# Softplus as one activation, and two complex sums formed on TensorE, in the third layer of a four-layer kernel

## The chip, the cores and the metric

The kernel runs on one core of a Trainium2 chip. The metric is the device time of one execution in microseconds; where several runs are given, their median. The engines are called PE (TensorE), DVE (VectorE), ACT (ScalarE), POOL (GpSimd) and SP (SyncE, which here only issues transfers).

## The reference, cut to what matters

The program runs four layers over x of shape (2, 128, 128, 128), each of the form x = x + layer(groupnorm(x)). The change is in the third (layer 2 in the code's numbering). With c = 64, x_r and x_i the two halves of the channels, and two filters A and B given as 7x7 kernels padded and taken to Fourier space:

```python
forget_gate = jax.nn.sigmoid(x_ri @ Wf + bf + 2.0)
input_gate = jax.nn.sigmoid(x_ri @ Wi + bi)
delta = jax.nn.softplus(x_ri @ Wd + bd) * 0.1
...
Bx_r = Br * x_r - Bi_ * x_i
Bx_i = Br * x_i + Bi_ * x_r
inp_r = delta[..., :c] * input_gate[..., :c] * Bx_r
inp_i = delta[..., c:] * input_gate[..., c:] * Bx_i
fg_r, fg_i = (forget_gate[..., :c], forget_gate[..., c:])
def step(h_state, _):
    h_r, h_i = h_state
    Ah_r = Ar * h_r - Ai * h_i
    Ah_i = Ar * h_i + Ai * h_r
    return ((fg_r * Ah_r + inp_r, fg_i * Ah_i + inp_i), None)
(h_r, h_i), _ = jax.lax.scan(step, h0, None, length=T)
```

T is 16. The kernel does not run the 16 steps: the recurrence is linear with constant coefficients for each element, so the sum of the 16 powers of a 2x2 matrix is built by repeated squaring.

## The kernel before, in words

Layer 2 goes through the 16384 positions of both images in 16 steps of 1024 positions. In a step the 128 partitions hold 64 channels of one half (r = 0 real, r = 1 imaginary, as an index in the free dimension) for two runs of 512 positions, and each big tile is 128 x [2 halves r, 2 images, 512], that is 2048 elements per partition; one half of it is 1024, and a tile without r is 1024 as well.

Each step has two parts. `front(i)` makes the gates (`gate`, matmuls into PSUM, then `gated`, an activation with bias per image), the filters (a1 to a11, with `kernels` on PE), the normalised input xn (n1), its product with B (v1 to v4) and with gate and softplus (d7, v5): the input v of the recurrence. `back(i)` forms the power sums on DVE with squares on ACT, and applies them: m1 is v times Ar with the crossed product m2 = v times Ai subtracted (half 0) or added (half 1), then multiplied by f and by b; hv is v times q. `last(r)` adds xh, hv and m1 on PE into PSUM (xs), ACT copies the sum to xh, `measure(r)` takes its statistics on DVE, and for r = 1 the step's result is stored and a later input is loaded by SP. These four end steps of step i run within back(i + 1).

Softplus is built from simple functions: e is |z| (d1), s is relu(z) (d2), e becomes exp(-e) (d3), up is 1 + e (d4), ln is log(up) (d5), c5 corrects e, and d6 adds s + ln - e on PE into the PSUM tile sp, which d7 reads.

The order of the work is written out by hand. `in_order` makes each engine run its instructions in the order in which they are emitted; between engines only data and buffers order them. The loop runs back(i) with front(i + 1) woven between its steps, one for one, and the first steps of front(i + 2) (`lead`) near the end. front returns a list; so does back, in the order of the list.

Buffers count. Pools `one`, `two`, `three` have as many buffers for each tag. PSUM has two buffers for the gates (l2gps), one for the filters aps and bps (l2aps) and one for everything in l2sps: sp0, sp1, xs0 and xs1 before. Among the SBUF tiles of pool `one`, up, xn and m2 share the tag l2up, and ln and hv share l2ln. A new tile of a full tag takes the place of the oldest and waits for that tile's readers.

Lines of the profile that matter: L883 gate, L890 gated, L873 kernels, L898/L901 and L904/L907 square, sum, root and the first use of it, L968 c5, L973 to L975 d6, L978 d7, L984 n1, L991/L994 v1 and v2, L997/L1000/L1003 v3, v4, v5, L1052 and L1061 m1 and m2, L1064 and L1068 the two half sums, L1069 the product with f, L1029 to L1032 last, L1036 measure, L1078 hv, L845/L847 load, L854 load_halves, L864 store.

Of the kernel before, what the change touches and what calls it, by code (L numbers as in the profile page):

```python
# [9 lines left out]
F32 = mybir.dt.float32  # L10
AF = mybir.ActivationFunctionType
ALU = mybir.AluOpType
# [3 lines left out]
P = 128  # L16
NB = 2
# [730 lines left out]
def layer2(tc, cs, ins, x2, x3, stats2, stats3):  # L748
# [7 lines left out]
    nc = tc.nc  # L756
# [3 lines left out]
    with ExitStack() as ctx:  # L760
        pool = lambda name, bufs, **kw: ctx.enter_context(tc.tile_pool(name=name, bufs=bufs, **kw))
        w = pool("l2_w", 1)
# [5 lines left out]
        for j, k in enumerate("fid"):  # L768
            nc.scalar.dma_start(wcat[:, j, :], ins[f"L2_conv_W{k}"])
            h = ins[f"L2_conv_b{k}"]  # L770
            for p0 in (0, HC):
                nc.scalar.dma_start(
                    bcol[p0 : p0 + HC, j, :], bass.AP(h.tensor, h.offset, [[1, HC], [HC, 2]])
                )
        one_col = w.tile([P, 1], F32, name="one_col")
        nc.gpsimd.memset(one_col, 1.0)
        eps_col = w.tile([P, 1], F32, name="eps_col")
        nc.gpsimd.memset(eps_col, 1e-8)
        minus = w.tile([P, P], F32, name="minus")
# [55 lines left out]
        def tile_of(i, name, shape, pl=one, tag=None):  # L835
            held.setdefault(i, {})[name] = t = pl.tile(shape, F32, name=f"{name}_{i}", tag=tag or f"l2{name}")
            return t
# [50 lines left out]
        def gated(i, j, r, out, func):  # L888
            for b in range(NB):
                A.activation(out[:, r, b], held[i][f"g{j}{r}"][:, b], func, bias=bias[:, b, j, r : r + 1])  # L890

        def front(i):

            h = lambda n: held[i][n]

            def a1():
                ps = kernels(i, 0, "aps")
                A.activation(tile_of(i, "sq", [P, 2, N]), ps, AF.Square)  # L898

            def a2():  # L900
                V.tensor_tensor(tile_of(i, "mag", H), h("sq")[:, 0], h("sq")[:, 1], ALU.add)  # L901

            def a3():
                A.activation(h("mag"), h("mag"), AF.Sqrt, bias=eps_col)  # L904

            def a4():
                V.tensor_scalar(tile_of(i, "rec", H), h("mag"), 1e-8, None, ALU.add)  # L907

            def a5():
                V.reciprocal(h("rec"), h("rec"))  # L910

            def a6():
                A.activation(h("mag"), h("mag"), AF.Sigmoid)

            def a7():
                V.scalar_tensor_tensor(h("rec"), h("mag"), 0.95, h("rec"), ALU.mult, ALU.mult)

            def a8():
                V.tensor_tensor(tile_of(i, "ar", [P, 2, N], two), h("aps"), over(h("rec"), 2), ALU.mult)

            def a9():
                A.activation(tile_of(i, "sq", [P, 2, N]), h("ar"), AF.Square)

            def a10():
                V.tensor_tensor(tile_of(i, "al", H, two), h("sq")[:, 0], h("sq")[:, 1], ALU.add)
                kernels(i, 1, "bps")

            def a11():
                A.copy(tile_of(i, "br", [P, 2, N]), h("bps"))

            def f1(r):
                if r == 0:
                    tile_of(i, "f", D, two)
                gated(i, 0, r, h("f"), AF.Sigmoid)

            def i1(r):
                if r == 0:
                    tile_of(i, "ig", D)
                gated(i, 1, r, h("ig"), AF.Sigmoid)

            def d1(r):
                if r == 0:
                    tile_of(i, "e", D)
                gated(i, 2, r, h("e"), AF.Abs)

            def d2(r):
                if r == 0:
                    tile_of(i, "s", D)
                gated(i, 2, r, h("s"), AF.Relu)


            def d3(r):
                if r == 0:
                    nc.scalar.preload_act_table_set("natural_log_exp_and_others")
                A.activation(h("e")[:, r], h("e")[:, r], AF.Exp, scale=-1.0)

            def d4(r):
                if r == 0:
                    tile_of(i, "up", D)
                A.activation(h("up")[:, r], h("e")[:, r], AF.Identity, bias=one_col)  # L960

            def d5(r):
                if r == 0:
                    tile_of(i, "ln", D)
                A.activation(h("ln")[:, r], h("up")[:, r], AF.Ln)

            def c5():
                V.scalar_tensor_tensor(h("e"), h("up"), -1.0, h("e"), ALU.add, ALU.subtract)  # L968

            def d6(r):  # L970
                ps = tile_of(i, f"sp{r}", W, ps_s, "l2sps")
                for b in range(NB):
                    nc.tensor.matmul(ps[:, b], cs.ident, h("s")[:, r, b], start=True, stop=False)  # L973
                    nc.tensor.matmul(ps[:, b], cs.ident, h("ln")[:, r, b], start=False, stop=False)
                    nc.tensor.matmul(ps[:, b], minus, h("e")[:, r, b], start=False, stop=True)  # L975

            def d7(r):
                V.scalar_tensor_tensor(h("ig")[:, r], h(f"sp{r}"), 0.1, h("ig")[:, r], ALU.mult, ALU.mult)  # L978

            def n1(r):  # L980
                if r == 0:
                    tile_of(i, "xn", D, tag="l2up")
                for b in range(NB):
                    A.activation(  # L984
                        h("xn")[:, r, b], h("xh")[:, r, b], AF.Identity,
                        scale=aff[:, r, b, 0:1], bias=aff[:, r, b, 1:2],
                    )


            def v1():  # L990
                V.tensor_tensor(tile_of(i, "v", D, two), h("xn"), both(h("br")[:, 0]), ALU.mult)  # L991

            def v2():
                V.tensor_tensor(h("xn"), h("xn"), both(h("br")[:, 1]), ALU.mult)  # L994

            def v3():
                V.tensor_tensor(h("v")[:, 0], h("v")[:, 0], h("xn")[:, 1], ALU.subtract)  # L997

            def v4():
                V.tensor_tensor(h("v")[:, 1], h("v")[:, 1], h("xn")[:, 0], ALU.add)  # L1000

            def v5():
                V.tensor_tensor(h("v"), h("v"), h("ig"), ALU.mult)  # L1003

            g = lambda j, r: (lambda: gate(i, j, r))
            k = lambda f, r: (lambda: f(r))
            return [
                g(2, 0), k(d1, 0), k(d2, 0), g(2, 1), k(d1, 1), k(d2, 1), k(d3, 0), k(d3, 1),
                k(d4, 0), k(d4, 1), k(d5, 0), k(d5, 1), g(1, 0), a1, c5, a2, k(d6, 0), a3, g(1, 1),
                a4, a6, k(i1, 0), a5, k(d7, 0), k(d6, 1), k(i1, 1), g(0, 0), a7, k(f1, 0), k(d7, 1),  # L1010
                a8, g(0, 1), a9, k(n1, 0), k(f1, 1), a10, a11, k(n1, 1), v1, v2, v3, v4, v5,
            ]

        def back(i):
# [7 lines left out]
            tt, stt = V.tensor_tensor, V.scalar_tensor_tensor  # L1022
            sq = lambda o, a: A.activation(o, a, AF.Square)
            M, AD, SU = ALU.mult, ALU.add, ALU.subtract

            def last(r):
                ps = tile_of(i, f"xs{r}", W, ps_s, "l2sps")
# [6 lines left out]
            def measure(r):  # L1034
# [24 lines left out]
                lambda: (tt(S, p, S, M), sq(q, p)),  # L1059
                lambda: (tt(u, d, u, M), sq(t2, u)),  # L1060
                lambda: tt(tile_of(i, "m2", D, tag="l2up"), x, both(ai), M),  # L1061
                lambda: tt(p, p, u, SU),
                lambda: stt(p, p, 1.0, b, AD, M),
                lambda: tt(v["m1"][:, 0], v["m1"][:, 0], v["m2"][:, 1], SU),  # L1064
                lambda: tt(b, p, q, AD),
                lambda: tt(q, q, d, M),
                lambda: (tt(u, q, t2, SU), sq(q, S), sq(t2, u)),
                lambda: tt(v["m1"][:, 1], v["m1"][:, 1], v["m2"][:, 0], AD),  # L1068
                lambda: tt(v["m1"], v["m1"], f, M),  # L1069
                lambda: tt(S, S, u, SU),  # L1070
                lambda: stt(S, S, 1.0, b, AD, M),
                lambda: tt(b, S, q, AD),
                lambda: tt(q, q, d, M),
                lambda: tt(q, q, t2, SU),
                lambda: tt(t, d, b, M),
# [14 lines left out]
        with in_order(tc):  # L1090
            load(0)
            load_halves(0)
            for i in range(-1, STEPS):
                if i + 2 < STEPS and i >= 0:
                    load(i + 2)
                elif i < 0:
                    load(1)
                    load_halves(1)
                    load_halves(2)

                ahead = [[f] for f in steps_of(i + 1)]
                lead = steps_of(i + 2)
                if i >= 0:
                    ahead[0:10] = [[] for _ in ahead[0:10]]
                if ahead:
                    ahead[-5][:0] = lead[0:6]
                    ahead[-1][:0] = lead[6:10]
                behind = back(i) if i >= 0 else []
                n = max(len(behind), 1)
                for j in range(n):  # L1110
                    if behind:
                        behind[j]()
                    for group in ahead[len(ahead) * j // n : len(ahead) * (j + 1) // n]:
                        for step in group:
                            step()
            for step in held[STEPS - 1]["end"]:
                step()
# [780 lines left out]
```

## Time and profile before

| | |
|---|---|
| Median of 3 runs | 18375.93 us (18361.79 to 18383.79) |
| Span of the profiled execution | 18336.7 us |
| What the median has beyond that span | 39.2 us |
| Layer 2 in the span | 4430 to 5540 us |
| Busy in it, of 1110 us | PE 678.76, DVE 1010.78, ACT 564.71, POOL 1.31 |
| Mean granted TensorE clock in it | 0.81 |

The profile is one execution; its span runs from the first to the last instruction. The page gives no device time of that execution beside the span, so the median of the runs stands for it. Over the whole span DVE is busy for 87%, ACT 81%, PE 78%; most of it is the fourth layer's scan, which the change does not touch. An operation's duration is the mean of its group; two instructions that follow each other on an engine overlap a little, so that start to start is some 0.1 us less than the duration, or just over it when the second needs the first's result.

### The profile page before, as it was taken

The page shows a single profiled execution, that of the slowest core. Times are in us where ns is not written, and L with a number is a line of the kernel's source. Part 1 is how long each engine was busy: PE and PEld are TensorE (multiplying, and loading weights), DVE is VectorE, ACT ScalarE, POOL GpSimd, SP SyncE. Part 2 cuts the span into 40 slices and gives each one's busy share as a digit, 9 for nine tenths or more (in the row PEclk, how much of TensorE's full clock was granted, in tenths as well). Part 3 has the DMA queues.
Part 4 walks back from the last instruction along what each step waited for, and adds up shares of the span by engine and source line. Part 5 has one row for each costly group of instructions (what it writes and reads, how often), then busy time and mean ns, then how long its engine had stood idle before and what let it go on. Part 6 is the DMA issues. An engine that isn't in the chain of part 4 may idle for free. (4 is left out here: it accounts for less than half of the span.)

```text
span 18336.7 us, 277675 instructions
## 1 busy us (share of the span) xinstructions
PE 14346.5 (78%) x97794; PEld 8284.5 (45%) x97794; DVE 15970.0 (87%) x20729; ACT 14905.8 (81%) x30049; POOL 11817.0 (64%) x6490
## 2 busy tenths in 40 slices
PE   7888888887668677777777777777777777777778
PEld 5555555664223344444444444444444444444445
DVE  6776666336999899999999999999999999999996
ACT  4665666334546799999999999999999999999984
POOL 0000000011000599999999999999999999999981
PEclk9999999889889899999999999999999999999989
DMA  2000000121115544444444455544444444445546
GB/s 45 23 24 23 17 18 16 61 65 56 56 51 191 155 116 116 121 127 127 125 116 116 118 127 129 128 121 115 116 125 128 129 125 117 116 119 127 127 131 192
DMA packets 1232638, 1859.32 MB, mean 101 GB/s; under 512 B 124877, under 2 KB 591565, under 8 KB 1228942
## 3 DMA queue, kind: packets, MB, share of 16 engines
q1 hardware_dynamic: 1157374, 1817.40, 37.6%
q10 hardware_dynamic: 73872, 24.16, 0.5%
q8 instruction: 776, 12.71, 0.3%
q14 instruction: 616, 5.05, 0.1%
HBM read 1396.64 MB, written 444.60 MB: 100 GB/s over the span
## 5 line engine op out<-in xcount | busy, mean ns | idle before, releaser
L1625 DVE TENSOR_TENSOR_SCAN hs<-da,states,ups 128x512 f32<-128x512 f32 x8192 | 9931.7, 1265 | 255.4 <-PE ups L1617 238.7
L1643 POOL TENSOR_TENSOR hs<-hs,cb 128x2048 f32<-128x2048 f32 x2048 | 9399.9, 4590 | 318.0 <-POOL but L1580 198.6
L1617 PE MATMUL ups<-ident,but 128*128 128x128 f32 x32768 | 5560.5, 301 | 2617.4 <-DVE hs L1625 1715.1
L1617 PEld LDWEIGHTS ups<-ident,but 128*128 128x128 f32 x32768 | 3859.2, 150 | 6207.6 <-DVE hs L1625 3515.8
L1585 ACT ACTIVATE but<-du,bt 128x256 f32<-128x256 f32 x12800 | 5350.7, 500 | 4.5 <-DVE du L1466 4.2
L1561 ACT ACTIVATE da<-db,na 128x512 f32<-128x512 f32 x8192 | 5238.6, 713 | 18.6 <-DMA db<-dd 15.8
L1599 PE MATMUL yps<-hs,sel 128*32 128x512 f32 x16384 | 2482.5, 682 | 50.4 <-POOL hs L1643 44.3
L1580 POOL TENSOR_TENSOR but<-du,bt 128x256 f32<-128x256 f32 x3584 | 2148.5, 619 | 17.0 <-DVE du L1466 17.0
L306 POOL TENSOR_TENSOR xres<-xres,rowb 128x256 f32<-128x256 f32 x128 | 94.3, 737 | 2440.3 <-DMA xres<-in_x 1744.7
L391 ACT COPY pT<-tps 128x512 f32<-128x512 f32 x1280 | 723.6, 585 | 1104.3 <-PE tps L386 1104.1
L386 PE MATMUL tps<-ident,s 128*128 128x128 f32 x8192 | 1223.7, 286 | 437.4 <-DVE pT L389 271.0
L358 DVE CUSTOM_DVE_ANT_1 s<-sps,relbias 128x512 f32<-128x512 f32 x2048 | 1321.7, 683 | 133.2 <-PE sps L341 127.9
L386 PEld LDWEIGHTS tps<-ident,s 128*128 128x128 f32 x8192 | 896.4, 143 | 1029.4 <-issue 498.5
L371 ACT ACTIVATE s<-s,nm 128x1024 f32<-128x1024 f32 x1024 | 1166.2, 1141 | 126.8 <-DVE nm L369 124.1
L1156 POOL MEMSET xpad<- 128x34 f32 x8 | 1.3, 162 | 1170.1 <-PE xs L1030 1105.8
L341 PE MATMUL sps<-kc,qT 32*128 32x512 f32 x4096 | 614.7, 668 | 1.9 <-DVE qT L326 1.2
L1637 ACT COPY states<-hs 128x4 f32<-128x4 f32 x2048 | 384.4, 188 | 247.5 <-DVE hs L1625 247.5
L389 DVE COPY pT<-tps 128x512 f32<-128x512 f32 x768 | 528.1, 688 | 55.9 <-PE tps L386 53.2
L1599 PEld LDWEIGHTS yps<-hs,sel 128*32 128x32 f32 x16384 | 339.4, 114 | 476.1 <-issue 301.9
L1349 PE MATMUL xdps<-xc,xpw 128*40 128x512 f32 x1024 | 540.8, 610 | 12.4 <-POOL xd L1286 12.4
L734 POOL TENSOR_TENSOR xr<-xr,row_ln_b 128x512 f32<-128x512 f32 x64 | 81.2, 1271 | 708.2 <-DMA xr<-x 474.7
L1381 PE MATMUL dtps<-xd,dtw 65*128 65x512 f32 x1024 | 534.0, 603 | 0.0
(287 smaller groups left out, 16171.3 us busy)
## 6 DMA issues: line engine op xcount, KB each, us to landing
db<-dd SPq DMA_DIRECT2D x1024, 512.0 KB
cb<-cd SPq DMA_DIRECT2D x1024, 256.0 KB
xc<-xs SPq DMA_DIRECT2D x256, 512.0 KB
dd<-dl SPq DMA_DIRECT2D x256, 512.0 KB
ut<-xst SPq DMA_DIRECT2D x128, 512.0 KB
yc<-ysb SPq DMA_DIRECT2D x128, 512.0 KB
yf<-yc SPq DMA_DIRECT2D x128, 512.0 KB
ys<-yt SPq DMA_DIRECT2D x128, 512.0 KB
```

Of the source, the lines that this page charges most:

```text
L341: nc.tensor.matmul(sps, v["qT"][hp, qt * P : (qt + 1) * P], kc[b, wh + g][hp, ww : ww + 2].rearrange("p a r c -> p (a r c)"), start=True, ...
L358: nc.vector.tensor_tensor_reduce(blocks(v["s", qt][:, h, 512 * g : 512 * g + 512]), blocks(v["sps", qt, g][h]), bias[:, h, :, r0 : r0 + WS ...
L371: nc.scalar.activation(s[:, h, :], s[:, h, :], AF.Exp, bias=nm[:, 2, h : h + 1], scale=-1.0, accum_out=v["sums"][:, qt, h : h + 1],)
L386: nc.tensor.transpose(tps[:, j, :], v["s", qt][:, h, k0 : k0 + P], cs.ident)
L391: nc.scalar.copy(dst, tps)
L1561: nc.scalar.activation(da[:, j, :], held[i]["db"][:, 4 * e + j, :], AF.Exp, scale=na[:, k, c : c + 1])
L1580: nc.gpsimd.tensor_tensor(but[:, j, :, n, :], du[:, tb], bt[:, tb, c : c + 1].unsqueeze(2).to_broadcast([P, 8, 32]), ALU.mult,)
L1585: nc.scalar.activation(but[:, j, :, n, :], du[:, tb], AF.Copy, scale=bt[:, tb, c : c + 1])
L1599: nc.tensor.matmul(v["yps"][e][32 * j : 32 * j + 32, :], sel, hs[:, j, :], start=(q == 0), stop=(q == 3),)
L1617: nc.tensor.transpose(ups[:, tb * P : (tb + 1) * P], v[("but", q, tb // 2)][:, tb % 2, 4 * e + j].rearrange("p n c -> p (n c)"), cs.ident,)
L1625: nc.vector.tensor_tensor_scan(o, a, u, state[:, c0 + j : c0 + j + 1], ALU.mult, ALU.add)
L1643: nc.gpsimd.tensor_tensor(hs, hs, v["cb"][:, s // 2, :].unsqueeze(1).to_broadcast([P, 4, T]), ALU.mult)
```

## The change

Softplus becomes one activation, AF.Softplus, written to e; d2 to d6, c5 and their tiles go, and d7 reads e from SBUF. A new helper `cross` forms a[r] -/+ b[1 - r] on PE: the identity times one half, and the identity or its negative times the other half of the crossed product, added in PSUM. v3 and v4 become vs(0), vs(1) with it, and the subtraction and addition on m1 become ms(0), ms(1). v5 and the product with f are done by halves, reading these PSUM tiles. kernels(i, 1) becomes a step of its own, kb, and both lists are put in a new order; the lead is now four steps, all at the end of the step.

```diff
-        one_col = w.tile([P, 1], F32, name="one_col")
-        nc.gpsimd.memset(one_col, 1.0)
...
+        def cross(i, name, a, b, r):
+            ps = tile_of(i, name, W, ps_s, "l2sps")
+            for n in range(NB):
+                nc.tensor.matmul(ps[:, n], cs.ident, a[:, r, n], start=True, stop=False)
+                nc.tensor.matmul(
+                    ps[:, n], cs.ident if r else minus, b[:, 1 - r, n], start=False, stop=True
+                )
...
             def a10():
                 V.tensor_tensor(tile_of(i, "al", H, two), h("sq")[:, 0], h("sq")[:, 1], ALU.add)
+
+            def kb():
                 kernels(i, 1, "bps")
...
             def d1(r):
                 if r == 0:
                     tile_of(i, "e", D)
-                gated(i, 2, r, h("e"), AF.Abs)
...
+                gated(i, 2, r, h("e"), AF.Softplus)
 
             def d7(r):
-                V.scalar_tensor_tensor(h("ig")[:, r], h(f"sp{r}"), 0.1, h("ig")[:, r], ALU.mult, ALU.mult)
+                V.scalar_tensor_tensor(h("ig")[:, r], h("e")[:, r], 0.1, h("ig")[:, r], ALU.mult, ALU.mult)
...
-            def v3():
-                V.tensor_tensor(h("v")[:, 0], h("v")[:, 0], h("xn")[:, 1], ALU.subtract)
-
-            def v4():
-                V.tensor_tensor(h("v")[:, 1], h("v")[:, 1], h("xn")[:, 0], ALU.add)
-
-            def v5():
-                V.tensor_tensor(h("v"), h("v"), h("ig"), ALU.mult)
+            def vs(r):
+                cross(i, f"vs{r}", h("v"), h("xn"), r)
+
+            def v5(r):
+                V.tensor_tensor(h("v")[:, r], h(f"vs{r}"), h("ig")[:, r], ALU.mult)
...
             return [
-                g(2, 0), k(d1, 0), k(d2, 0), g(2, 1), k(d1, 1), k(d2, 1), k(d3, 0), k(d3, 1),
-                k(d4, 0), k(d4, 1), k(d5, 0), k(d5, 1), g(1, 0), a1, c5, a2, k(d6, 0), a3, g(1, 1),
-                a4, a6, k(i1, 0), a5, k(d7, 0), k(d6, 1), k(i1, 1), g(0, 0), a7, k(f1, 0), k(d7, 1),
-                a8, g(0, 1), a9, k(n1, 0), k(f1, 1), a10, a11, k(n1, 1), v1, v2, v3, v4, v5,
+                g(2, 0), k(d1, 0), g(2, 1), k(d1, 1), g(1, 0), a1, a2, a3, g(1, 1),
+                a4, a6, k(i1, 0), a5, k(d7, 0), k(i1, 1), g(0, 0), a7, k(f1, 0), k(d7, 1),
+                a8, kb, k(n1, 0), a11, k(n1, 1), v1, v2, k(vs, 0), g(0, 1), a9, k(f1, 1),
+                k(v5, 0), k(vs, 1), a10, k(v5, 1),
             ]
...
+            def ms(r):
+                cross(i, f"ms{r}", v["m1"], v["m2"], r)
+
+            def mf(r):
+                tt(v["m1"][:, r], v[f"ms{r}"], f[:, r], M)
...
                 lambda: tt(tile_of(i, "m2", D, tag="l2up"), x, both(ai), M),
-                lambda: tt(p, p, u, SU),
+                lambda: (ms(0), tt(p, p, u, SU)),
                 lambda: stt(p, p, 1.0, b, AD, M),
-                lambda: tt(v["m1"][:, 0], v["m1"][:, 0], v["m2"][:, 1], SU),
                 lambda: tt(b, p, q, AD),
                 lambda: tt(q, q, d, M),
                 lambda: (tt(u, q, t2, SU), sq(q, S), sq(t2, u)),
-                lambda: tt(v["m1"][:, 1], v["m1"][:, 1], v["m2"][:, 0], AD),
-                lambda: tt(v["m1"], v["m1"], f, M),
+                lambda: (mf(0), ms(1)),
                 lambda: tt(S, S, u, SU),
                 lambda: stt(S, S, 1.0, b, AD, M),
                 lambda: tt(b, S, q, AD),
+                lambda: mf(1),
...
                 if i >= 0:
-                    ahead[0:10] = [[] for _ in ahead[0:10]]
+                    ahead[0:4] = [[] for _ in ahead[0:4]]
                 if ahead:
-                    ahead[-5][:0] = lead[0:6]
-                    ahead[-1][:0] = lead[6:10]
+                    ahead[-1][:0] = lead[0:4]
```

More of the change, by code (lines that the diff above doesn't have):

```diff
@@ L943, in d1 @@
                     tile_of(i, "e", D)
-                gated(i, 2, r, h("e"), AF.Abs)
[L946 to L975, printed above, removed]
+                gated(i, 2, r, h("e"), AF.Softplus)
             def d7(r):
-                V.scalar_tensor_tensor(h("ig")[:, r], h(f"sp{r}"), 0.1, h("ig")[:, r], ALU.mult, ALU.mult)
+                V.scalar_tensor_tensor(h("ig")[:, r], h("e")[:, r], 0.1, h("ig")[:, r], ALU.mult, ALU.mult)
             def n1(r):
```

## The prediction

> **What bounds the kernel now.** I read the windows view first, because the change lies in the third layer alone: its instructions run from 4430 to 5540 us of the span.
>
> ```profile
> core 0: us, PE busy (x) PEld busy (x) DVE busy (x) ACT busy (x) POOL busy (x), PEclk, DMA share, GB/s
> 4430.00:5540.00 1110.00, 678.76 (x1824) 242.68 (x1824) 1010.78 (x784) 564.71 (x688) 1.31 (x7) 0.81 0.18 51
> ```
>
> This stage is 1110 us, 6% of the span, and DVE is busy for 1011 of them; PE and ACT have room. What counts is therefore DVE's queue: the instructions on it and the times it waits. The waits of the same window say who makes DVE wait (waited for, by whom: total, times, longest), and what PE waits for:
>
> ```profile
> PE xs L1030 <- DVE hv L1078: 215.2, 16, 28.3
> ...
> DVE ig L978 <- PE sp L975: 28.1, 16, 5.0
> ...
> DVE rec L907 <- ACT mag L904: 13.5, 16, 1.3
> DVE mag L901 <- ACT sq L898: 12.1, 8, 1.7
> ```
>
> Leaving out the first step's shares (4.98, 1.34 and 0.51 us), a steady step has 23.1/15 + 12.2/15 + 11.6/15 = 3.1 us of DVE waits. Steps begin 65.4 and 67.7 us apart in turn (hv L1078 starts at 4606.76, 4672.19, 4739.88), 66.6 on average. PE spends 12 us a step waiting for DVE. The groups of the window give the prices (form, count, busy, mean ns):
>
> ```profile
> L968 DVE SCALAR_TENSOR_TENSOR e<-up,e 128x2048 f32<-128x2048 f32 x16 | 36.6, 2285 | 13.9 <-ACT up L960 13.9
> ...
> L997 DVE TENSOR_TENSOR v<-v,xn 128x1024 f32<-128x1024 f32 x16 | 19.5, 1220 | 0.0
> L919 DVE TENSOR_TENSOR ar<-aps,rec 128x1024 f32<-128x1024 f32 x16 | 19.5, 1218 | 0.0
> ...
> L954 ACT ACT_TABLE_LOAD x16 | 20.5, 1283 | 0.3
> ```
>
> Last, the timeline of PE around one restart, and the waits of the DMA queue:
>
> ```profile
> 4742.22 2.07 PE L1030 MATMUL xs<-hv,ident 128*128 128x512 f32 x2 [12.21 <-DVE hv L1078]
> 4744.09 1.91 PE L1031 MATMUL xs<-m,ident 128*128 128x512 f32 x2
> 4745.80 1.51 PE L1029 MATMUL xs<-xh,ident 128*128 128x512 f32 x2
> 4747.14 1.02 PE L1030 MATMUL xs<-hv,ident 128*128 128x512 f32 x2
> ```
>
> ```profile
> SPq L847 <- PE bps L873: 816.9, 15, 64.0
> ```
>
> A pair of 128x512 records costs 0.86 us from start to start at full clock (4747.14 to 4748.00) and 1.7 to 1.9 when the granted clock is 0.50, as after this 12 us gap. The queue line shows a rule of this program: a tile whose tag has one buffer (tab) is not written until the last reader of the tile it replaces is done, even where that reader (bps) is emitted later than the request.
>
> **What leaves DVE.** Per step c5 (L968) and the four half sums v3, v4, L1064, L1068 go: start to start 2.20 + 1.14 + 1.26 + 1.13 + 1.22 = 6.9 us. v5 and the multiplication by f become two halves each, about 0.1 us more per pair. That a sum is read from PSUM costs nothing: L919 reads PSUM at 1218 ns, L997 reads SBUF at 1220. d7 now reads SBUF: 1.19 to 1.22. Net -6.8. The old 3.1 us of waits go too: sp exists no longer, and mag and rec get new places.
>
> **What leaves ACT and PE.** ACT loses Relu, Exp, Identity and Ln, 9.4 us a step by the means of their groups (716 ns x4, 1050 x2, 1143 x2, 1055 x2), but is busy only half the time: nothing by itself. Softplus takes the place of Abs (701 ns), same form, PSUM source and bias. Table loads stay three a step, each 1.283 us: softplus, square root, sigmoid, where it was log/exp, square root, sigmoid. If softplus could not share its table with Copy and Square it would be one more; on the path that matters only between the copy of xs1 and the root, 1.3 us a step, 14 x 1.3 = 18 us. PE loses 24 records of sp and gains 32 of the four cross products, with 12 us of slack a step. The memset and kernels(1) as its own step kb cost nothing: kb still runs between a8 and a11 with 4 us to spare, and SP's tab load, which waits for it, comes no later.
>
> **Where DVE waits after the change.** All six uses of the one l2sps buffer (xs0, xs1, ms0, ms1, vs0, vs1) now follow each other: each waits until the one before is read. I wrote out the order in which each engine gets its instructions and followed it with the row durations. Four places wait.
>
> W1, square root's input. PE's queue from the end of v5(0) is vs1, the next step's g20 and g21, xs0 of the step just ended, g10, aps. At full clock: 4 pairs 3.44 + two gates 3.5 (8 records took 1.77) + 6 pairs 5.15 + 1.75 + 1.75 + 0.2, then ACT's square 1.01 + 0.1: 16.9 us. DVE has beside it qq, hv, a10, v5(1), t, two products and d, two stats: 11.1 us, and then stands at mag (a2). Wait 5.8. Before, hv alone released xs0, and the gates stood ahead of it.
>
> W2, rec (a4). From a2's start, DVE has 0.6 + 2.20 + 1.25 + 1.25 = 5.3. ACT's queue: the copy of xs1 stands ahead of the root. xs1 ends 4.1 us after a2 starts (5.15 + 0.2 from the end of aps, 1.2 of which lie before a2); copy 1.01, table load 1.28, root 0.72: 7.2. Wait 1.9.
>
> W3, v1. m2 and xn share one buffer (tag l2up). In the old order m2's last reader was L1068, a DVE instruction placed ahead of n1. Now it is ms1 on PE, which waits for mf(0) to read ms0, and n1(0) stands before ms1 in the text but, by the tab line, must wait for it. Behind n1(0) on ACT stand a11 and n1(1), and v1 needs all three. From the end of mf(0): ms1 3.44 + 0.2, n1 1.43, br 0.92, n1 1.51, 0.2: 7.6; DVE has only two 1.2 us instructions. Wait 5.2.
>
> W4, v5(0). vs0 starts after mf(1), when PE has idled some 11 us, so at half clock: two to four of its pairs at 1.7, 5.2 to 6.9 with latency, against 5.7 us of DVE work. 0 to 1.2; I take 0.5, since the quoted restart had three slow pairs.
>
> [...]
>
> [...]
>
> **Sum.** Waits 5.8 + 1.9 + 5.2 + 0.5 = 13.4; less 3.1 of old waits and 6.8 of work: +3.5 us a step. 14 full steps give +49. The first front has no cover: its c5, v3, v4 and the 4.98 us wait for sp go (9.7), two crosses on the chain come (at most 5): -5. The last step has no next front: two half sums go, -2. Total +42, rounded to +40: the same walk of the old order gives steps of 65.3 and 67.9 us where the trace has 65.4 and 67.7, so a tenth or two a step stays open. The profiled span is 18336.7; the median is 18375.9, so 39.2 us lie around it, unchanged. 18376.7 of span, 18416 us in all, +0.22%.
>
> **Rivals.** A, about no change: W3 is not paid in full, for instance if n1 finds its buffer free. Without W3 a step is 3.5 - 5.2 = -1.7, at most 14 x -1.7 - 7 = -31; part comes back, because vs0 then starts earlier after less cover: about 18360. For it: the walk has slack that I cannot see. Against: the tab line.
>
> B, faster: DVE stays the only bound and every wait is hidden, since PE has 12 us of idle a step. The 6.8 us of DVE work go 16 times: 18376 - 109 = 18267. It decides if PE's queue runs ahead of DVE by over 6 us at v5(1), that is if the gates did not stand between vs1 and xs0. Against: one buffer forbids running ahead.
>
> [...]
>
> **How the numbers follow.** About 0.2% (37 us) is what a measurement of this kernel tells from no change, so the forecast, at +40, lies just over the line. Forecast 0.60 (0.48 above the line, 0.12 below), A 0.21, B 0.12, C 0.07. Slower 0.48 + 0.07 = 0.55, same 0.12 + 0.21 = 0.33, faster 0.12. The forecast's own range, W1 and W3 each off by one microsecond, W4 between its bounds, is 18385 to 18445. With most of A the range is 18360 to 18448, leaving out B and C, 0.19.
>
> **What would show it.** DVE waits at mag behind the square of aps (about 4 us after a stats wait of 2), at rec behind the root (1.9), at v1 behind xn (5.2), a little at v5(0). hv's starts 70 us apart. ACT waits for PE's ms1 at n1. Softplus at 0.7 us, three loads a step. If v1 does not wait and hv stands 66 us apart, A is right; at 60, B.

## The result, and the profile after

The changed kernel takes 18467.18 us (median of 4 runs, 18447.94 to 18475.81) against 18379.86 us for the kernel before beside it (4 runs, 18361.79 to 18410.53): a ratio of 1.0049, 95% interval 1.0034 to 1.0063. It is slower by 87 us. The forecast was slower by 40 us with a range up to 18448: the sign was right, the size was short by half.

Where the time lies can be read from two marks that both kernels have: the bias of the second image, with which the third layer's steps can begin, and the last statistics. "The layer" is the time between them in what follows. It is 1105.4 us before and 1168.1 us after; in a second profile of each, 1104.2 and 1169.1. So the layer is 63 to 65 us longer. The other 22 to 24 us lie outside it. In the profiles what is longer behind the layer is the fourth layer's scan, which the change does not touch (by 42 us in the first pair of profiles, by 25 in the second); the last experiments return to it.

The windows view of the changed kernel over exactly its layer (time, then busy us of PE, PEld, DVE, ACT and POOL with counts, granted clock, DMA share, GB/s):

```profile
4455.70:5623.80 1168.10, 776.06 (x1920) 266.40 (x1920) 902.96 (x731) 436.28 (x528) 0.50 (x5) 0.81 0.17 48
```

DVE's busy time falls as forecast: by the same view over the layer of the kernel before it is 1009.22 us, now 902.96, 6.6 us less a step. But DVE's idle time in the layer rises from 96 to 265 us. Who makes it wait stands in the waits view (waited for, by whom: total, times, longest):

```profile
PE vs L893 <- DVE m L1004: 162.2, 15, 10.8
...
DVE v L968 <- ACT xn L961: 85.2, 16, 6.2
...
DVE stats L1016 <- ACT xh L1012: 71.3, 17, 8.4
...
DVE mag L907 <- ACT sq L904: 44.5, 16, 9.2
ACT xn L961 <- PE ms L894: 44.5, 15, 3.0
...
DVE rec L913 <- ACT mag L910: 29.5, 15, 2.0
...
DVE v L977 <- PE vs L894: 27.3, 32, 4.6
```

The four DVE instructions that the prediction named are all there: v1 (L968), mag (L907), rec (L913) and v5 (L977). The line with stats is a part of W1's wait, as the timeline of one steady step shows (start, duration, instruction, and in brackets the idle time ahead and who ended it):

```profile
4838.28 1.22 DVE L977 TENSOR_TENSOR v<-vs,ig 128x1024 f32<-128x1024 f32 x1 [1.15 <-PE vs L894]
...
4840.67 2.29 DVE L1057 TENSOR_TENSOR hv<-v,q 128x2048 f32<-128x2048 f32 x1
...
4843.78 1.23 DVE L977 TENSOR_TENSOR v<-vs,ig 128x1024 f32<-128x1024 f32 x1 [0.22 <-PE vs L894]
...
4853.75 1.30 DVE L1016 BATCH_NORM_STATS2 stats<-xs 128x6 f32<-128x512 f32 x2 [3.97 <-ACT xh L1012]
4857.42 0.69 DVE L907 TENSOR_TENSOR mag<-sq 128x512 f32<-128x512 f32 x1 [2.37 <-ACT sq L904]
...
4864.72 0.43 DVE L913 TENSOR_SCALAR rec<-mag 128x512 f32<-128x512 f32 x1 [2.01 <-ACT mag L910]
...
4896.30 2.29 DVE L968 TENSOR_TENSOR v<-xn,br 128x2048 f32<-128x2048 f32 x1 [5.29 <-ACT xn L961]
...
4912.34 2.29 DVE L1057 TENSOR_TENSOR hv<-v,q 128x2048 f32<-128x2048 f32 x1
```

From hv to hv (L1057) the step takes 71.67 us. Its waits are 5.29 at v1, 1.15 + 0.22 at the halves of v5, 3.97 + 2.37 at stats and mag, and 2.01 at rec: 15.0 us, where the prediction had 13.4. With 66.6 - 3.1 - 6.8 + 15.0 = 71.7 the step adds up; no other term is needed.

The timeline of PE shows the restart that was costed from the old trace:

```profile
4831.55 2.04 PE L893 MATMUL vs<-v,ident 128*128 128x512 f32 x2 [10.81 <-DVE m L1004]
4833.39 1.91 PE L894 MATMUL vs<-xn,minus 128*128 128x512 f32 x2
4835.09 1.92 PE L893 MATMUL vs<-v,ident 128*128 128x512 f32 x2
4836.80 1.44 PE L894 MATMUL vs<-xn,minus 128*128 128x512 f32 x2
4838.17 1.94 PE L881 MATMUL g<-xT,wg 128*64 128x512 f32 x8
4840.04 1.12 PE L893 MATMUL vs<-v,ident 128*128 128x512 f32 x2
```

After 10.81 us without work not only three but all four pairs of vs0 run slowly. The fourth takes 1.37 us to the next start, between a slow pair's 1.71 and a fast one's 0.86, so that full clock came back within it. The granted clock (the number behind POOL's count) in the windows view puts that at 4837.64, 6.1 us after the restart:

```profile
4831.55:4837.64 6.09, 6.09 (x7) 2.49 (x8) 5.55 (x4) 0.00 (x0) 0.00 (x0) 0.50 0.01 3
4837.64:4868.30 30.66, 25.83 (x82) 8.92 (x80) 21.32 (x20) 15.62 (x19) 0.00 (x0) 1.00 0.11 34
```

From the groups (form, count, busy us and mean ns, idle time ahead):

```profile
L888 ACT ACTIVATE e<-g,bias 128x512 f32<-128x512 f32 x64 | 40.5, 684 | 53.3 <-PE g L881 53.3
```

Softplus is a single activation of 684 ns; the same view has three groups of 16 table loads, three a step as before, at 1283 ns each. A half of v5, which reads PSUM, takes 1224 ns (L977).

### The profile page after: what moved, and what is told of

Read it like the earlier page. It is cut to its first block, busy times and chain, and to the rows that moved or that the text cites. A ratio compares the mean times of both kernels' runs of the same rounds, so it can differ in the third digit from the quotient of the medians.

```text
span 18461.4 us, 277738 instructions
## 1 busy us (share of the span) xinstructions
PE 14513.0 (79%) x97922; PEld 8345.4 (45%) x97922; DVE 15880.8 (86%) x20681; ACT 14741.1 (80%) x29889; POOL 11821.4 (64%) x6489
```

## The experiments

Five kernels undo one thing each or do one part alone, one joins three of these, and three move the scan that follows. Layer and steps are from the profile of each; the times are medians with the number of runs, against the kernel before on the same chip in the same hour. The kernels before and after were also profiled once more.

> The kernel before once more, for its profile. The two profiles at hand differ by 125 us of span, but only 63 us of it lie between the first gate matmul and the last statistics of the third layer; 22 lie in the two layers before it and 40 in the fourth, which the change does not touch. Theory S (scatter): these 62 us are how executions differ, and a second profile of the kernel before shows its third layer within 2 us of the first one's 1105 us, with steps of 65.4 and 67.7 us, while the other layers move by tens of us. Rival F (far effect): the change slows the other layers, and this profile agrees with the first one in every layer within 5 us.

> The changed kernel once more. Theory S: third layer 1168 us again, steps of 71.68 us; the other layers within the scatter of the kernel before; time 65 to 90 us above the kernel before. Rival F: the fourth layer again 40 us longer than in every profile of the kernel before.

| kernel | median us (runs) | before | ratio, 95% interval | layer us | steady step us |
|---|---|---|---|---|---|
| before, again | 18363.81 (1) | 18355.92 | | 1104.2 | 65.42 and 67.69 in turn |
| after, again | 18447.94 (4) | 18355.92 | 1.0050 (1.0035 to 1.0065) | 1169.1 | 71.68 |
| own_buffer | 18348.49 (10) | 18355.92 | 0.9997 (0.9988 to 1.0007) | 1116.6 | 68.27 |
| softplus_only | 18385.83 (10) | 18355.92 | 1.0014 (1.0005 to 1.0023) | 1109.8 | 68.27 |
| gates_early | 18326.99 (10) | 18375.44 | 0.9976 (0.9967 to 0.9985) | 1068.4 | 64.85 |
| root_first | 18388.12 (10) | 18375.44 | 1.0008 (0.9999 to 1.0017) | 1096.7 | 66.03 and 67.10 in turn |
| keep_warm | 18439.09 (4) | 18375.44 | 1.0039 (1.0025 to 1.0053) | 1144.0 | 69.85, at times 70.2 |
| all_three | 18249.69 (5) | 18375.44 | 0.9932 (0.9919 to 0.9946) | 981.9 | 58.4 to 60.5 |

Two profiles of one kernel agree in the layer to 1.2 us, so the layer column separates the kernels far better than the medians do. Outside the layer they agree less: in the second profile of the kernel before the third layer begins 26 us later than in the first, and in that of the changed kernel the scan is 16 us shorter than in the first. So theory S holds for the layer, and rival F, 40 us more in the fourth layer each time, does not: it is 42 and then 25. The time, 92 us above the kernel before, is just over the 65 to 90 of theory S.

**A buffer of its own for xn** (W3). Only the tag of xn is changed, so that n1 need not wait for ms1, the last reader of m2:

```diff
-                    tile_of(i, "xn", D, tag="l2up")
+                    tile_of(i, "xn", D)
```

> The changed kernel with xn in a buffer of its own, so that n1 need not wait for ms(1). Theory W (waits along the one order): the 5.3 us wait of v1 behind xn goes and the others stay, at most 1 or 2 us of it come back at v5(0), because the cover before it is shorter; steps of 66.5 to 68.5 us, 45 to 70 us faster than the changed kernel, that is 15 us on either side of the kernel before. Rival R (the clock's raster): the step sits at 71.68 us, 21 times 3.413 us, because the granted clock changes only at such marks; it goes to a whole number of marks, 68.27 us if one is gained, else it stays. Rival P (PE is full): taking the wait away gives nothing, as PE's queue is the bound.

The layer falls from 1169 to 1117 us, still 11 us above the kernel before, and the time is level with it. The step of 68.27 us lies in theory W's range and is also rival R's mark, so this run does not decide between the two. DVE's waits, in the waits view from 4600 to 5400 us (12 steps):

```profile
DVE v L968 <- ACT xn L961: 26.3, 12, 2.2
...
DVE v L977 <- PE vs L894: 11.8, 24, 0.8
```

v1's wait falls from 5.29 to 2.19 a step, by 3.1 and not by 5.2. The rest has another cause, which the timeline of ACT shows:

```profile
4804.53 1.06 ACT L997 ACTIVATE q<-S 128x1024 f32<-128x1024 f32 x1 [8.79 <-DVE u L1046]
...
4806.44 1.51 ACT L961 ACTIVATE xn<-xh,aff 128x512 f32<-128x512 f32 x2
```

n1 (L961) no longer waits for PE, but starts directly behind two squares of back(i), and these stand in ACT's queue behind DVE's u (8.79 us of idle). The buffer was the wait that came last; the place in ACT's queue is the next one. The shared tag costs 3.4 us a step (71.68 to 68.27) and 52 us of the layer. Of the 3.4 us, 3.1 come at v1 and 0.3 at v5 (1.38 to 1.06), because vs0's slow stretch is 5.6 us here instead of 6.1 by the granted clock.

**The gate and the lead earlier** (the part of W1 that the gates add, and W4). The gate g01 with its two users is issued before v1 instead of behind vs0, and the lead (the first four steps of the front after next) six groups of steps earlier:

```diff
-                a8, kb, k(n1, 0), a11, k(n1, 1), v1, v2, k(vs, 0), g(0, 1), a9, k(f1, 1),
-                k(v5, 0), k(vs, 1), a10, k(v5, 1),
+                a8, kb, k(n1, 0), a11, k(n1, 1), g(0, 1), a9, k(f1, 1), v1, v2, k(vs, 0),
+                k(v5, 0), k(vs, 1), a10, k(v5, 1),
...
-                    ahead[-1][:0] = lead[0:4]
+                    ahead[-7][:0] = lead[0:4]
```

> The changed kernel with its last gate (g01, with its sigmoid f1) and the four lead steps (both softplus gates of the next step) moved from around vs(1) into PE's 10.8 us pause before vs(0). Theory W: the two gates (3.5 us) leave the chain from v5(0) to mag, and vs(0) no longer starts cold, which takes the 1.2 + 0.2 us at v5: 71.68 - 4.9 = 66.8 us a step, 70 us faster than the changed kernel; the wait of v1 (5.3) stays. With the raster the step settles on the mark below, 64.85, or on 68.27. Rival P (what counts is the number of matmuls, or the one buffer): no change, since not one matmul or buffer is taken away.

The layer is 1068.4 us, 101 less than after the change, and the kernel is faster than before by 0.24% (0.15 to 0.33). The waits in the same view:

```profile
DVE mag L907 <- ACT sq L904: 28.4, 12, 2.4
...
DVE stats L1016 <- ACT xh L1012: 23.0, 13, 1.8
DVE v L968 <- ACT xn L961: 18.1, 12, 1.5
```

Stats waits 1.8 us a step instead of 4.0, v1 1.5 instead of 5.3, v5 0.4 instead of 1.4; mag and rec are as they were. Since an issue order was moved, several things move at once: the gates no longer stand between vs1 and xs0, g01 fills a part of PE's pause, and v1 comes later against the rest of back(i). This run shows what the order is worth in all, not how it divides among the three. The expectation had v1 keep its wait; it lost 3.8 us of it, so the step reached 64.85, the mark named, by another sum than the one expected. This is the largest gain of the five.

**The root ahead of xs1's copy** (W2). end[2], which issues xs1 and its copy, moves two places down:

```diff
                 end[1],
-                end[2],
                 lambda: tt(tile_of(i, "m1", D, two), x, both(ar), M),
                 lambda: tt(u, u, d, SU),
+                end[2],
```

> The changed kernel with the copy of xs1 placed behind the square root on ACT (end step 2 two places later in the list; PE's order stays). Theory W: only W2 goes, the 2.0 us of rec behind mag: 69.7 us a step, 28 us faster in all; on the raster either 71.68 (nothing) or 68.27 (48 us). The waits at mag (2.4), v1 (5.3) and the stats (4.0) stay. Rival P: nothing.

The wait at rec is gone from the view, and with it nearly all of mag's, which was not meant:

```profile
DVE v L968 <- ACT xn L961: 64.6, 12, 7.3
...
DVE mag L907 <- ACT sq L904: 2.1, 12, 0.2
```

mag waits 0.18 us a step instead of 2.37. In DVE's timeline m1's product (L1031, 2.27 us) now stands between the stats and mag, where it covers the rest of the chain through xs0, g10, aps and the square; in ACT's, the root comes before the copy of xs1. Two terms of the prediction, W2 and the end of W1, thus hang on one position in the list. v1 keeps its wait (5.2 in the steady steps). The steps, 66.03 and 67.10 in turn, are below all that was expected, since mag's wait went as well. The layer is 1096.7 us, below that of the kernel before, yet the median is 13 us above it (0.9999 to 1.0017, no verdict): in the profile the scan is 11707 us here, against 11675 and 11676 in the kernel before.

**PE kept busy in its pause** (W4). The gate g01 is computed five more times into its own PSUM tile before vs0, work without use, there to keep the clock up:

```diff
-                a8, kb, k(n1, 0), a11, k(n1, 1), v1, v2, k(vs, 0), g(0, 1), a9, k(f1, 1),
+                a8, kb, k(n1, 0), lambda: (a11(), again(i, 0, 1, 5)), k(n1, 1), v1, v2, k(vs, 0),
+                lambda: again(i, 0, 1, 1), a9, k(f1, 1),
```

(again issues the eight matmuls of the gate so many times.)

> The changed kernel with nothing moved; g01 is computed five more times into its own PSUM tile in PE's 10.8 us pause before vs(0) (the last time where it stood), work for nothing, so that PE does not stand still there. Theory C (clock): vs(0) then runs at full clock, 3.6 instead of 6.7 us; the waits at v5 (1.2 and 0.2) go and the step falls by 1.4 us or to the next mark: 70.3 or 68.27 us, 20 to 48 us faster with 40 more matmul records a step. Rival P: PE's queue is the bound, and 8.7 us of matmuls more make the step longer by as much. Rival N: the clock plays no part, nothing changes.

PE's timeline in this kernel:

```profile
4814.49 8.80 PE L893 MATMUL g<-xT,wg 128*64 128x512 f32 x40
4825.37 2.04 PE L905 MATMUL vs<-v,ident 128*128 128x512 f32 x2 [2.08 <-DVE m L1017]
4827.21 1.79 PE L906 MATMUL vs<-xn,minus 128*128 128x512 f32 x2
4828.84 1.02 PE L905 MATMUL vs<-v,ident 128*128 128x512 f32 x2
```

The pause ahead of vs0 is 2.08 us instead of 10.81, two pairs are slow instead of four, and DVE has no wait left at v5. In this step vs0 takes 5.3 us up to g01's start, which DVE's own work covers. By the windows view from 4600 to 5500 us the mean granted clock is 0.90, against 0.81 in the changed kernel. Steps take 69.96 us on average (979.45/14) instead of 71.6; the waits at v1, stats, mag and rec hardly change (5.19, 3.97 or 3.79, 2.37, 2.01). So the slow stretch of vs0 costs 1.65 us a step, 24 us of the layer, which is then 39 us longer than before.

**Softplus alone.** The single activation stays; v3, v4, v5 and the two half sums return to DVE as before:

```diff
-            def vs(r):
-                cross(i, f"vs{r}", h("v"), h("xn"), r)
+            def v3():
+                V.tensor_tensor(h("v")[:, 0], h("v")[:, 0], h("xn")[:, 1], ALU.subtract)
...
-                lambda: (mf(0), ms(1)),
+                lambda: tt(v["m1"][:, 1], v["m1"][:, 1], v["m2"][:, 0], AD),
+                lambda: tt(v["m1"], v["m1"], f, M),
```

> The kernel before with softplus as one activation and nothing on PE for the sums (v3, v4, v5 and the two half sums on DVE as before; kernels(1) stands behind a10 as before; the first four steps of the next front where the first six stood). By DVE's queue alone each step loses c5 (2.2 us) and the waits for sp (1.5): 62.9 us a step, 55 us faster than before. Theory R (raster): PE now has long pauses, restarts at half clock, and the step settles on a multiple of 3.413 us: 68.27 us, slower than before by about 10 us in all, although work left every engine. If so, half of the loss of the change is not in the crosses. Rival Q: softplus as an activation is slower than 0.7 us or needs a fourth table load.

Taking c5 and the wait for sp from DVE does not make the layer shorter (1109.8 against 1104 to 1105 us), for a new wait takes their place:

```profile
DVE mag L907 <- ACT sq L904: 76.3, 12, 6.6
```

mag waits 6.4 us a step. Its input comes through aps, and in this shorter list aps stands behind xs1's six pairs in PE's queue, where after the whole change it stands ahead of them. The step was expected at 68.27 and is 68.27, though the expectation did not rest on this wait. A restart at half clock, which it did name, stands in the same chain, at the head of xs0:

```profile
4817.61 2.07 PE L1012 MATMUL xs<-hv,ident 128*128 128x512 f32 x2 [14.92 <-DVE hv L1060]
```

Its first three pairs take 5.2 us to the next start (4822.78) instead of three times 0.86, so the restart can account for up to 2.6 us of the 6.4, an estimate; no run took the two apart. What follows is bounded: softplus in this place in the order brings nothing. That it would bring nothing in any order was not tried.

**The three repairs together:** own buffer, gates early and root first.

> Own buffer for xn, gates early and root first together. Theory W: of the waits 5.3 (v1), 2.0 (rec), 1.4 (v5) and 3.5 of the 6.4 (stats and mag) go: 71.68 - 12.2 = 59.5 us a step, or 61.44 us (18 marks) on the raster; 140 to 170 us faster than the changed kernel, 18280 to 18310 us, so about 60 us below the kernel before. DVE would then be busy nearly throughout. Rival P: not below the kernel before, since the crosses on PE cost what they save on DVE.

This kernel is faster than either theory had it: 18249.69 us, 0.68% faster than before (0.54 to 0.81). Its steps, 59.2 us on average, are near the 59.5 of theory W's sum and do not settle on the 61.44 of the raster. The windows view over its layer, and DVE's waits from 4600 to 5400 us:

```profile
4467.10:5449.00 981.90, 736.64 (x1920) 249.79 (x1920) 898.83 (x730) 433.34 (x528) 0.50 (x5) 0.89 0.20 57
```

```profile
DVE stats L1016 <- ACT xh L1012: 24.8, 14, 1.8
DVE m L1004 <- PE ms L894: 8.9, 8, 2.1
DVE mag L907 <- ACT sq L904: 2.3, 13, 0.2
DVE v L977 <- PE vs L894: 2.0, 1, 2.0
```

DVE's busy time is that of the changed kernel (898.83 against 902.96 us), and the layer is 186 us shorter. Of 15.0 us of waits a step some 2.8 are left (38.0 us in the 13.5 steps of the view). So the edits to the arithmetic do pay, once little waits for them. A better order alone could not have done it: the kernel before has 63 us of DVE work in a step (1009.22/16), more than the 59.2 us that a step takes here.

**Does the scan's time hang on its start?** The scan of the fourth layer takes 11674.7 and 11676.0 us in the two profiles of the kernel before, 11716.2 and 11700.5 in those after. All other stages behind the layer agree within 3 us. Three kernels add 14 or 28 additions on DVE behind the third layer:

```diff
             for step in held[STEPS - 1]["end"]:
                 step()
+            for _ in range(14):
+                V.tensor_tensor(held[STEPS - 1]["hv"], held[STEPS - 1]["hv"], held[STEPS - 1]["m1"], ALU.add)
```

> The kernel before with 14 additions of 128x2048 on VectorE after the last step of the third layer (on tiles that nobody reads again), about 14 x 2.2 = 31 us that only delay what follows. Question: why the fourth layer's scan, which no kernel here touches, takes 11674.7 and 11676.0 us in the two profiles of the kernel before, 11716.2 and 11700.5 in those of the changed one, and 11661.8 to 11708.2 in the others. Theory P (the scan's length hangs on the moment at which it starts): the scan leaves 11674 to 11677 by 8 us or more. Theory Q (it hangs on what the third layer leaves behind, its program or its tiles): the scan stays within 11674 to 11677, and the whole is 18376 + 31 = about 18407 us.

> As the kernel with 14 additions, with 28 of them: about 62 us of delay, which brings the scan's start to about where it is in the changed kernel. Theory P: the scan differs from 11675 by 8 us or more, and from that of the kernel with 14 additions. Theory Q: it stays within 11674 to 11677, the whole about 18438 us.

> The changed kernel with the same 14 additions (31 us) after its third layer. Theory P: the scan leaves 11700 to 11716. Theory Q: it stays within 11700 to 11716, the whole about 18464 + 31 = 18495 us.

| kernel | median us (runs) | before | delay us | scan us |
|---|---|---|---|---|
| before + 14 | 18392.13 (10) | 18366.23 | 32 | 11672.3 |
| before + 28 | 18428.01 (6) | 18366.23 | 65 | 11646.1 |
| after + 14 | 18470.45 (4) | 18366.23 | 31 | 11694.0 |

Neither theory holds as it was put. A start 32 us later leaves the scan of the kernel before alone (11672.3), one 65 us later gives a scan 29 us shorter in the profiled execution, and the changed kernel's, 31 us later, is 6 us below the lower of its two others. But the execution with the scan 29 us shorter, at 18391.9 us, is the shortest of six; the other five lie between 18419.78 and 18438.67, which fits a scan of the usual length. So executions of this one program differ by 28 to 47 us, and in the profiled one it is the scan that is short, while its third layer is as long as ever (1105.7 us). The two layers ahead scatter as well: the third begins between 4433.9 and 4467.1 us over all the profiles, with no relation to the kernel. By medians the changed kernel has 22 to 27 us outside the layer in two comparisons and 8 in the third (18470.45 - 18366.23 - 65 - 31). Over the variants of the changed kernel the scan runs from 11661.8 (own_buffer) to 11708.2 us (keep_warm). What makes it longer, and whether it always is, stays open; the profiles do not show that the change does it.

## Why the prediction was right or wrong, point by point

Measured in the steady step of the changed kernel, in us:

| step of the prediction | forecast | measured |
|---|---|---|
| work off DVE | -6.8 | -6.6 by busy time of the layer, -6.8 by step and waits |
| W1, stats and mag | 5.8 | 6.3 |
| W2, rec | 1.9 | 2.0 |
| W3, v1 | 5.2 | 5.3 |
| W4, v5 | 0.5 (0 to 1.2) | 1.4 |
| all waits | 13.4 | 15.0 |
| step against before | +3.5 | +5.1 |
| first front | -5 | -6 |
| last step | -2 | -2 and 0 in the two pairs of profiles |
| layer | +42, rounded to +40 | +63 to +65 |
| outside the layer | 0 | +22 to +24 |

**Right:** the mechanism, and all four places. W3 rested on one line of the DMA queue's waits (816.9 us in 15 waits), which showed that in this program a tile of a full tag waits for a reader that is issued later. It is the longest wait at one instruction; own_buffer shows that the tag is 3.1 us of it, and that the rest has another wait right behind it. W2 and W3 came out to 0.1 us from row durations and a written order (W3's terms add up to 7.7 and not 7.6, which makes it the 5.3 measured). Softplus at 0.7 us (684 ns), three loads of 1283 ns and the cost of reading PSUM (1224 ns for a half of v5) were as costed. ACT hardly stands idle ahead of a load: at the root and the sigmoid there are 16 loads each with 0.3 us of idle time ahead in total.

**Wrong, the term of the sum that was mis-sized: W4.** It was bounded at 0 to 1.2, for two to four slow pairs, and set to 0.5, for the three of the one restart quoted, where full clock came back after 4.55 us. In the steady step v5(0) waits 1.15, the upper bound, and v5(1) another 0.22: vs0 is four pairs long and lies wholly inside a slow stretch of 6.1 us. The length of this stretch is not fixed. Over the runs it goes from 3.4 (keep_warm) to 6.2 us (root_first), and the wait at v5 goes with it (the stretch is counted from vs0's start until the granted clock is full again; the first step is that between the first two hv):

| run, step | vs0 at half clock, us | wait at both halves of v5, us |
|---|---|---|
| root_first, every other steady step | 3.54 | 0.22 |
| own_buffer, first step | 4.67 | 0.57 |
| changed kernel, first step | 5.24 | 0.94 |
| own_buffer, steady step | 5.62 | 1.06 |
| root_first, the steps between | 5.80 | 1.19 |
| changed kernel, steady step | 6.11 | 1.38 |

For a stretch of 4.55 us the 0.5 was thus about right; what failed was to take the length from one restart. In the trace of the kernel before, others lasted 4.0 and 5.7 us. W4 is 0.9 of the 1.6 us that the waits of a step are over the forecast, 12 us of the layer.

Half a microsecond more, 7 us of the layer, is **W1**. Its chain was let start at the end of v5(0), but g01 stands between vs0 and vs1 in PE's queue: v5(0) ends at 4839.50, vs1 starts at 4840.04. This is not an effect of the clock, for in keep_warm stats and mag wait 3.97 and 2.37 us as well. That run takes the waits at v5 away, and the step falls to 69.96 us, where the forecast with W4 at nothing would be 69.6. The 24 us of the layer that it saves are what vs0's slow stretch costs in all, of which the forecast had 7.

**Wrong in a detail that cost nothing:** W1's split. The forecast had 2 us at stats and 4 at mag; it is 3.97 and 2.37. The statistics of xs start only when ACT's copy of the same PSUM tile has ended (copy at 4852.71 for 1.01 us, stats at 4853.75), which the walk let run side by side. mag waits for PE's chain anyway, so the sum of both is what the chain gives.

**Wrong, without effect on the difference:** the 39.2 us put "around the span". The profiled execution of the changed kernel took 18463.18 us with a span of 18461.4: 1.8 us lie around a span. The rest was the difference between two executions.

**Wrong, a term put at nothing without a reason:** the time outside the layer. The sum adds the layer's 40 us to the span and leaves the rest as it was. There lie 22 to 24 of the 47 us that the forecast falls short by, as much as the layer's terms together, and with the layer's 63 to 65 us alone the time would have been inside the range. No run shows what causes it. The range allowed for none of it, since it was made of the layer's terms alone, although the three times before already spread over 22 us. It was also added up too narrow: W1 and W3 off by 1 us each and W4 at its bounds, all at once, make 18381 to 18454, not 18385 to 18445.

**The rivals.** A (W3 not paid in full) fell: n1 waits 3.0 us on ACT for ms1, and v1 5.3. own_buffer is what A supposed, and it lands near A's no change (18348, ratio 0.9997), but not by A's sum: that had a step 1.7 us shorter than before, and it is 1.7 longer, the layer 11 us longer. B (all waits hidden) was to be decided by whether PE runs ahead of DVE at v5(1); the change does not let it. all_three, with three things changed, comes to 18250, near B's 18267. C (a cold restart in W1's chain) fell: PE does not idle before vs1, and the one restart that DVE waits for is vs0's, which the forecast had itself as W4.

## What to carry to other kernels

When sums move from VectorE to TensorE, write down every engine's queue in the new order, and cost each tile's wait for the last reader of the tile whose buffer it takes, even where that reader is issued later: here 6.6 us of VectorE work saved a step became 5 us lost, and one tag alone cost 3.4 of them. Before such a change is given up, move the waiting work in the queues; the same arithmetic with one buffer more and three places in the order changed is 0.7% faster than the kernel before. A short TensorE job behind a long pause is costed by the longest slow stretch that the traces show (6.2 us here), not by one example, and together with what stands between it and the next job that counts. And terms "outside the change" get a width from repeated runs, not nothing.

## What the runs showed of the hardware that was not expected

The granted clock changes between 0.50 and 1.00 on a raster of 3.413 us over the whole execution: the traces of the kernels before and after record 1024 and 1086 stretches at one of the two, and the distance from the start of one to that of the next is a multiple of 3.4133 us, to within 0.001 us. The third layer's steps settle on multiples of it: 71.68 us is 21 times 3.413, 68.27 (own_buffer, softplus_only) is 20, 64.85 (gates_early) is 19, and the alternating pairs of the kernel before (67.69 + 65.43) and of root_first make 133.1 us, which is 39. The changed kernel reaches its value from below: 71.14, 71.41, 71.55, 71.65, 71.67, then 71.68 to the end. Its slow stretches at vs0 grow alongside, 5.24, 5.77, 6.03, 6.09, then 6.11 us, and each ends on a mark.

The likely reason, the author's estimate from these figures, is this. A step shorter than 71.68 us lets the next restart begin earlier before its mark; the slow stretch up to the mark is longer, and so is the step, until it is 21 marks long. The two kernels that have no wait at v5 in the steady steps do not settle on one mark: keep_warm takes 69.96 us on average, 20.5 marks, and all_three 58.4 to 60.5 us. No run was made to test this by itself. A saving inside such a step can then count for more or less than its own size: in own_buffer v1's wait falls by 3.1 us and the step by 3.4.

That a stretch can be longer than 3.413 us is also to be read in the trace. In the steady step of the changed kernel vs0 begins at 4831.55, 2.7 us before a mark, and PE is busy from there on; by the windows view the clock is 0.50 up to this mark (4834.23), 0.50 for the 3.41 us up to the next one (4837.64) and 1.00 for the 3.41 us behind that. In the kernel before, the stretches at half clock behind the restarts of the steady steps lasted 4.0 to 5.7 us. What decides at which mark the clock rises is not shown by these runs.
